# Cross attention with eight-slot batches: residual rows in four buffers loaded one per slot, and all query-weight sums on GpSimd

## The chip, the cores and the metric

The kernel runs on one core of one Trainium2 chip. The metric is device time in microseconds (us), the median of several executions. The core has five instruction queues that run beside each other and wait for one another by semaphores: TensorE (PE, matrix products into PSUM), VectorE (DVE), ScalarE (ACT), GpSimd (POOL) and SyncE (SP). In this kernel almost every DMA is issued by SP. Each queue is worked off in its order.

## The reference

All is float32: x is 8 x 256 x 1024, the context is 8 x 256 x 1024, there are 32 heads of width 32.

```python
residual = x
h = (x - mean(x)) * rsqrt(var(x) + 1e-5) * ln_gamma + ln_beta
Q = split_heads(h @ Wq.T)                       # 32 heads of 32
K = V = split_heads(ctx)
scores = where(mask, einsum(Q, K) / sqrt(32), -inf)
attn = einsum(softmax(scores), V)
out = residual + merge_heads(attn) @ Wout.T
```

## The kernel before

**Slots.** The work is cut into 64 slots, n = 0 to 63: eight per batch (NQ = 8), each with four heads. The main loop (line 828) writes the instructions of each slot in a fixed order; nothing reorders them afterwards. In slot n TensorE does the scores of slot n + 1 (`scores`, L469), the product of probabilities and values of slot n - 2 (`values`, L599), a part of the query projection of a later batch (L330 and, from batch 3 on, L430), and a part of the output projection of the batch before (L661). The softmax of slot n + 1 runs beside it: VectorE adds the mask bias and takes the minimum (L503), ScalarE takes the exponential (L507), VectorE the reciprocal of the sum (L514), GpSimd multiplies (`normalize`, L516, 8 instructions a slot), VectorE transposes by blocks (`blocks`, L522), ScalarE copies a part (L528), and SP moves blocks between partitions (L579, L583). I write b for the batch whose output is projected and i for the place in its eight slots: n = 8(b + 1) + i.

**Output projection with seven products.** The output of a batch is made by a Strassen-like scheme of seven products (`PRODUCTS`, L624) instead of eight, 28 matmuls in all, spread over the slots by `STEPS` (L631; the last such batch by `ENDS`). All go to one PSUM bank, since `ps_o` has one buffer. The first product, A11 with B11, is copied aside (`keep_p1`, L669). After A12 with B21 has been added, the bank is added to the residual rows (0,0) and stored: `store`, L682 on VectorE and L683 on SP, in slot i = 2. Only then may the next product that begins the bank, S2 with T2, start on TensorE. In the same way `store(1, 0)` in slot 6 comes before the product S1 with T1. `take` (L678) adds the bank to other residual rows in slots 3 and 4, and GpSimd adds the first product to three of the four residual tiles (`add_p1`, L673, in slots 2 to 4). In the batch that `ENDS` governs (slots 56 to 63) the additions to the residual stand ahead of the slot's softmax; otherwise they are hooks within the softmax, after its eight L503 (hook 0) or a little later (hook 1).

**Residual rows.** A residual tile is 128 rows by 512 columns of x, 256 KB, read from DRAM by `load_res` (L148) into the pool `rp`, which has three buffers. The four tiles of a batch are called (s, h). The loads are put into the list `between`, which SP issues within the slot's tail between the two pairs of probability moves. With three buffers a load waits until the tile three places before has been stored:

```python
for s, h in {1: ((0, 0), (0, 1)), 2: ((1, 1),), 3: ((1, 0),)}.get(i, ()):
    between.append(partial(load_res, b, s, h))
```

**Query weights.** From batch 3 (`SPLIT`) the query projection also uses seven products. Its combined weights T1 to T4 are made once, in slots 9 to 21, from the blocks of Wq by 16 additions of 128 x 512 (`sum_wq`, L381), eight on GpSimd and eight on VectorE. T1 goes into the tile `ring`; T3, T2 and T4 replace blocks of `wq` that are used up. B11, T1 and T3 are written to DRAM (`keep_wq`, L387 and L390) and loaded into `ring` in every later batch (`load_ring`, L397). The same kind of sums for the output weights, `sum_wo` (L183), is on GpSimd.

**The rest.** `load_mask` (L189) and `mask_bias` (L459) prepare one batch's mask, each with two buffers. `sum_at` (L651) and `sum_x` (L420) are the GpSimd sums on the data side of the seven products.

Of the kernel before, what the change touches and what calls it, by code (L numbers as in the profile page):

```python
# [46 lines left out]
F32 = mybir.dt.float32  # L47
U8 = mybir.dt.uint8
# [3 lines left out]
P = 128  # L52
# [7 lines left out]
def xattn_kernel(  # L60
# [11 lines left out]
    nc = tc.nc  # L72
    B, S, D = x.shape
    T = mask.shape[2]
    HD = D // HEADS
    NC = D // P
    NQ = NC
# [10 lines left out]

    const = ctx.enter_context(tc.tile_pool(name="const", bufs=1))
    xp = ctx.enter_context(tc.tile_pool(name="xp", bufs=2))  # L90
    rp = ctx.enter_context(tc.tile_pool(name="rp", bufs=3))
    lnp = ctx.enter_context(tc.tile_pool(name="lnp", bufs=2))
    kp = ctx.enter_context(tc.tile_pool(name="kp", bufs=2))
    vp = ctx.enter_context(tc.tile_pool(name="vp", bufs=2))
# [5 lines left out]
    sm = ctx.enter_context(tc.tile_pool(name="sm", bufs=8))  # L100
# [4 lines left out]
    ps_q = ctx.enter_context(tc.tile_pool(name="ps_q", bufs=1, space=PS))  # L105
    ps_o = ctx.enter_context(tc.tile_pool(name="ps_o", bufs=1, space=PS))

    ident = const.tile([P, P], F32, tag="ident", name="ident")
    make_identity(nc, ident)
    mhalf = const.tile([P, NS], F32, tag="mhalf", name="mhalf")  # L110
    nc.gpsimd.memset(mhalf, -0.5)
# [34 lines left out]
    def load_res(b, s, h):  # L146
# [5 lines left out]
    gs = const.tile([P, NC], F32, tag="gs", name="gs")  # L152
    qa = const.tile([P, NQ, S + 1], F32, tag="qa", name="qa")
    wq = const.tile([P, NC, NC, P], F32, tag="wq", name="wq")
    NK = NC // 2
    ring = const.tile([P, NK, NK, P], F32, tag="ring", name="ring")
    sums_x = const.tile([P, 2, NK, NA, K], F32, tag="sx", name="sx")
    kept = {
        name: dram.tile([P, NK, NK * P], F32, tag=name, name=f"kept_{name}")
        for name in ("T1", "B11", "T3")  # L160
    }
    wo = const.tile([P, 7, NK, 512], F32, tag="wo", name="wo")
    B11, B21, B22, T1, T2, T3, T4 = range(7)
# [5 lines left out]
    def load_wo(which, pair):  # L169

        k, h = {B11: (0, 0), B21: (1, 0), B12: (0, 1), B22: (1, 1)}[which]
        rows = woT[ds((NK * k + 2 * pair) * P, 2 * P), ts(h, 512)]
        nc.sync.dma_start(
# [11 lines left out]
    mks = {}  # L185

    def load_mask(b):
        mks[b] = sm.tile([P, T], U8, tag="mk", name=f"mk_{b}", bufs=2)
        nc.sync.dma_start(mks[b], mask[:, b].to_broadcast([P, T]))  # L189

    nc.scalar.dma_start(gam, gamma)
# [4 lines left out]
    load_wq(0)  # L196
    load_k(0)
    load_mask(0)
    load_x(1, 0)
    load_wq(1)  # L200
# [162 lines left out]
    SPLIT = 3  # L363
    SOON, LATE = 0, NK
    W_AT = {"B12": (SOON, 0), "B22": (SOON, NK), "B11": (LATE, 0), "B21": (LATE, NK),
            "T2": (SOON, 0), "T3": (SOON, 0), "T4": (LATE, 0)}

    def weights(name, o):

        if name == "ring":  # L370
            return ring[:, o]
        first, k = W_AT[name]
        return wq[:, first + o, ds(k, NK)]

    def sum_wq(to, o, engine):

        to, a, b, op = {
            "T1": ("ring", "B12", "B11", ALU.subtract), "T3": ("T3", "B22", "B12", ALU.subtract),
            "T2": ("T2", "T3", "B11", ALU.add), "T4": ("T4", "B21", "T2", ALU.subtract),
        }[to]  # L380
        engine.tensor_tensor(weights(to, o), weights(a, o), weights(b, o), op)  # L381

    def keep_wq(name, half):

# [69 lines left out]
    mbs, scs, pTs, pvs, ats, pos = {}, {}, {}, {}, {}, {}  # L454

    def mask_bias(b):

        mbs[b] = sm.tile([P, T], F32, tag="mb", name=f"mb_{b}", bufs=2)
        nc.vector.tensor_scalar(mbs[b], mks.pop(b), 1.0, -MASKED, ALU.subtract, ALU.mult)  # L459

    def scores(n, part=range(NS)):
# [182 lines left out]
    def sum_at(b, name):  # L644
        if name == "S2":
            s2s[b] = up.tile([P, NK, P], F32, tag="s2", name=f"s2_{b}")
        one, two, op = {
            "S3": ("A11", "A21", ALU.subtract), "S2": ("A22", "S3", ALU.subtract),
            "S1": ("S2", "A11", ALU.add), "S4": ("A12", "S2", ALU.subtract),
        }[name]  # L650
        nc.gpsimd.tensor_tensor(operand(b, name), operand(b, one), operand(b, two), op)  # L651
# [54 lines left out]
    for n in range(N):  # L706
# [8 lines left out]
    loads, stats, norms, trans, moves, biases, masks = (  # L715
        {n: [] for n in range(N)} for _ in range(7)
    )
    for b in range(1, B):
        first = NQ * (b - 1) + 2
        if b == 1:  # L720
            when = dict(moves=())
        elif b == 2:
            when = dict(
                loads=(0, 1), stats=(2, 3), norms=(3, 3), trans=(4, 4),
                moves=tuple(4 + i // 4 for i in range(16)),
            )
        else:
            when = dict(
                loads=(first - 12, first - 11), stats=(first - 10, first - 9),
                norms=(first - 8, first - 7), trans=(first - 7, first - 6),  # L730
                moves=tuple(first - 5 + i // 6 for i in range(16)),
            )
        for table, key in (
            (loads, "loads"), (stats, "stats"), (norms, "norms"), (trans, "trans"),
        ):
            for i, n in enumerate(when.get(key, ())):
                assert n < first
                table[n].append((b, i))
        for n in range(N):
            part = [i for i, slot in enumerate(when["moves"]) if slot == n]  # L740
            if part:
                assert n < first - 1
                moves[n].append((b, part))
        biases[NQ * b - 3].append(b)
        masks[NQ * b - 5].append(b)


    sums = {n: [] for n in range(N)}
    for n, which, *chunks in (
        (3, T3, 0), (4, T3, 1), (5, T2, 0), (6, T2, 1), (7, T3, 2), (8, T3, 3), (8, T2, 2),  # L750
        (9, T2, 3), (11, T4, 0, 1), (12, T4, 2, 3), (12, T1, 0), (13, T1, 1, 2), (14, T1, 3),
    ):
        sums[n] += [partial(sum_wo, which, c) for c in chunks]
    for n, which, o, engine in (
        (9, "T1", 0, nc.gpsimd), (12, "T1", 1, nc.vector), (13, "T1", 2, nc.vector),
        (14, "T1", 3, nc.gpsimd), (14, "T3", 0, nc.gpsimd), (14, "T3", 1, nc.vector),
        (15, "T3", 2, nc.gpsimd), (15, "T3", 3, nc.vector), (16, "T2", 0, nc.gpsimd),
        (17, "T2", 1, nc.vector), (19, "T2", 2, nc.gpsimd), (19, "T2", 3, nc.vector),
        (20, "T4", 0, nc.gpsimd), (20, "T4", 1, nc.vector), (21, "T4", 2, nc.gpsimd),
        (21, "T4", 3, nc.vector),  # L760
    ):
        sums[n].append(partial(sum_wq, which, o, engine))


    away, rings = {n: [] for n in range(N)}, {n: [] for n in range(N)}
    for n, name, half in (
        (9, "B11", 0), (10, "B11", 1), (13, "T1", 0), (15, "T1", 1), (15, "T3", 0), (16, "T3", 1),
    ):
        away[n].append(partial(keep_wq, name, half))
    for n, b in firsts.items():  # L770
# [14 lines left out]
    ln_norm(0, 1, nc.vector)  # L785
    first_q(0, early + late)
    mask_bias(0)
    transpose_x0(1)
    scores(0, (0,))
# [19 lines left out]
    for b in range(B - 1):  # L809
        done, ends = 0, b == B - 2  # L810
        for i, counts in enumerate(ENDS if ends else STEPS):
            n = NQ * (b + 1) + i
# [15 lines left out]
    for n in range(N):  # L828
        b, i = divmod(n - NQ, NQ)
        new_q = new_qs[n]  # L830
        between = []
# [3 lines left out]
            between.append(partial(load_k, n + 4))  # L835
        between += rings[n]
        if b >= 0:
            for s, h in {1: ((0, 0), (0, 1)), 2: ((1, 1),), 3: ((1, 0),)}.get(i, ()):
                between.append(partial(load_res, b, s, h))
        between += [partial(load_x, *args) for args in loads[n]]  # L840
        between += [partial(load_mask, one) for one in masks[n]]
        if n < NQ:
            which, pair = (
                (B12, 0), (B22, 0), (B11, 0), (B12, 1), (B22, 1), (B11, 1), (B21, 0), (B21, 1)
            )[n]
# [54 lines left out]
        for one in biases[n]:  # L900
            mask_bias(one)
        project_steps(n, 2)
        if b >= 0:
            for name in {0: ("S3",), 2: ("S4",), 4: ("S1",)}.get(i, ()):
                sum_at(b, name)
        for slot, name in ((n + 2, "S1"), (n + 1, "S2"), (n + 1, "S4"), (n - 1, "S3")):
            if slot in firsts:
# [12 lines left out]
        if not new_qs[n] and n - 2 > N - NQ:  # L920

            chunks = [c for c in range(NQ) if N - NQ + c <= n - 3]
# [65 lines left out]
```

## Time and profile before

| | |
|---|---|
| median of 3 runs | 637.47 us (635.39 to 637.86) |
| the profiled execution, its time | 635.33 us |
| its span in the trace | 633.5 us |
| mean granted TensorE clock in it | 0.967 |
| busy: PE | 587.1 us (93%) |
| busy: DVE | 468.1 us (74%) |
| busy: ACT | 411.6 us (65%) |
| busy: POOL | 381.6 us (60%) |
| residual loads, issue to landing, median | 4.7 us by the list of issues |

Busy time of an engine is the time in which it worked on an instruction; a wait is idle time just before an instruction, and the profile names what released it. All durations come from the one profiled execution, whose time is 1.8 us above its span and 2.1 us below the median. The clock row of the profile gives the share of full TensorE speed that was granted in each fortieth of the span (15.8 us each).

### The profile page before, as it was taken

To read this page: it belongs to the slowest core of one execution; us is meant where nothing else is said; L and a number is where in the kernel's file an instruction comes from. 1 tells how busy PE (TensorE), PEld (TensorE's weight loads), DVE (VectorE), ACT (ScalarE), POOL (GpSimd) and SP (SyncE) were. 2 spreads that over 40 slices of the span, in tenths; PEclk is the share of its full clock that TensorE was granted. 3 is DMA by queue.
4 is the path that set the end of the run, shared out by engine and by line. 5 is a ranking of instruction groups with operands and counts; after the bars stand their busy time and mean duration, and the time that the engine had idled before them with its cause. 6 is when DMAs were issued, how large, how long until landed. Compare 5 with 4: busy or idle time off the path is not lost.

```text
span 633.5 us, 19986 instructions
## 1 busy us (share of the span) xinstructions
PE 587.1 (93%) x7160; PEld 399.5 (63%) x7160; DVE 468.1 (74%) x1698; ACT 411.6 (65%) x1420; POOL 381.6 (60%) x651
## 2 busy tenths in 40 slices
PE   8999999798999999799997999799997999958897
PEld 7787685465666766477665777457764676624343
DVE  6878777789868887688786888668765677748801
ACT  4778875775667676687747866677655766636710
POOL 1667976797587945765467734776446554546500
PEclk9999799999999999899998999989998999969899
DMA  8566786655876668576766678755766664446441
GB/s 317 184 200 187 189 250 173 213 165 155 227 246 187 190 189 241 174 220 196 207 205 178 188 215 234 216 159 155 192 178 211 205 166 127 142 134 184 114 139 66
DMA packets 48483, 119.02 MB, mean 188 GB/s; under 512 B 10240, under 2 KB 10240, under 8 KB 48384
## 3 DMA queue, kind: packets, MB, share of 16 engines
q1 hardware_dynamic: 48096, 117.74, 62.7%
q8 instruction: 57, 0.93, 0.7%
q14 instruction: 42, 0.34, 0.2%
q10 hardware_dynamic: 288, 0.01, 0.0%
HBM read 66.33 MB, written 11.53 MB: 123 GB/s over the span
## 4 chain that ended last, share of the span: by engine, by line
PE 54%; POOL 14%; DMA 10%; DVE 9%; issue 6%; ACT 4%; SPq 3%; DVEq 0%; POOLq 0%; ACTq 0%
PE po_S L661 14%; PE pq_A L430 13%; POOL e L516 10%; PE sc L469 7%; PE pv L599 6%; PE po_A L661 4%; DVE e L503 4%; DMA r<-in_x_dram 4%; PE po L690 3%; PE pq L330 3%; PE pq_S L430 3%; DMA pT<-pc 2%; ACT e L507 2%; DVE pT L522 2%; SPq L579 2%
## 5 line engine op out<-in xcount | busy, mean ns | idle before, releaser
L516 POOL TENSOR_SCALAR e<-e,rden 128x256 f32<-128x256 f32 x512 | 236.1, 478 | 174.2 <-DVE rden L514 171.8
L507 ACT ACTIVATE e<-e,mn 128x256 f32<-128x256 f32 x512 | 254.0, 501 | 60.0 <-DVE mn L503 57.9
L522 DVE STREAM_TRANSPOSE pT<-e 128x512 f32<-128x512 f32 x256 | 180.8, 707 | 44.6 <-POOL e L516 33.9
L503 DVE CUSTOM_DVE_ANT_0 e<-sc,mb 128x256 f32<-128x256 f32 x512 | 185.1, 416 | 37.5 <-PE sc L469 37.5
L528 ACT COPY pc<-pT 128x512 f32<-128x512 f32 x128 | 79.1, 618 | 94.8 <-DVE pT L522 52.3
L507 ACT ACTIVATION_READ_ACCUMULATOR e<-e,mn 128x1 f32 x512 | 98.1, 192 | 0.0
L661 PE MATMUL po_S<-wo,s 128*128 128x512 f32 x112 | 64.5, 708 | 34.3 <-DVE rden L514 24.2
L330 PE MATMUL pq<-xnT,wq 128*128 128x256 f32 (+1 forms) x368 | 86.2, 389 | 1.2 <-ACT qa L337 1.2
L661 PE MATMUL po_S<-wo,at 128*128 128x512 f32 x168 | 81.7, 606 | 1.8 <-DVE r L678 1.8
L330 PEld LDWEIGHTS pq<-xnT,wq 128*128 128x128 f32 x368 | 70.2, 194 | 16.4 <-issue 3.9
L599 PE MATMUL pv<-pT,v 64*32 64x128 f32 x4096 | 75.7, 276 | 2.6 <-ACT qa L339 1.4
L469 PE MATMUL sc<-k,qa 32*128 32x256 f32 x1024 | 77.3, 412 | 0.1
L469 PEld LDWEIGHTS sc<-k,qa 32*128 32x128 f32 x1024 | 48.1, 190 | 46.2 <-issue 27.1
L599 PEld LDWEIGHTS pv<-pT,v 64*32 64x32 f32 x4096 | 58.1, 106 | 28.7 <-issue 15.9
L661 PEld LDWEIGHTS po_S<-wo,s 128*128 128x128 f32 x112 | 22.4, 220 | 57.5 <-issue 51.1
L661 PE MATMUL po_A<-wo,at 128*128 128x512 f32 x112 | 53.2, 609 | 0.2 <-ACT qa L339 0.2
L514 DVE RECIPROCAL rden<-den 128x2 f32<-128x2 f32 x256 | 38.2, 149 | 20.1 <-ACT e L507 18.4
L661 PEld LDWEIGHTS po_S<-wo,at 128*128 128x128 f32 x168 | 28.6, 190 | 25.0 <-issue 22.0
L503 DVE DVE_READ_ACCUMULATOR2_ANT mn<- 128x1 f32 x512 | 42.1, 82 | 0.0
L430 PEld LDWEIGHTS pq_A<-xnT,wq 128*128 128x128 f32 x320 | 37.3, 192 | 4.8 <-issue 4.8
L430 PE MATMUL pq_A<-xnT,wq 128*128 128x128 f32 x320 | 37.3, 275 | 0.0
L661 PEld LDWEIGHTS po_A<-wo,at 128*128 128x128 f32 x112 | 19.7, 189 | 22.0 <-issue 19.9
(77 smaller groups left out, 588.9 us busy)
## 6 DMA issues: line engine op xcount, KB each, us to landing
v<-in_kv_dram SPq DMA_DIRECT2D x32, 512.0 KB, 4.1
pT<-pT SPq DMA_DIRECT2D x128, 128.0 KB, 2.4
pT<-pc SPq DMA_DIRECT2D x128, 128.0 KB, 4.5
ring<-kept_T SPq DMA_DIRECT2D x18, 512.0 KB, 6.0
k<-in_kv_dram SPq DMA_DIRECT2D x32, 256.0 KB, 3.3
x<-in_x_dram SPq DMA_DIRECT2D x14, 512.0 KB, 6.0
r<-in_x_dram SPq DMA_DIRECT2D x28, 256.0 KB, 4.7
out_dram<-r SPq DMA_DIRECT2D x28, 256.0 KB, 3.3
```

The costliest lines, as they stand in the source:

```text
L330: nc.tensor.matmul(pqs[n], wq[:, o, c, :], xnTs[b](c), start=(c == 0), stop=(c == NC - 1),)
L430: nc.tensor.matmul(pqs[b][:, o, :], w[:, c], x_[:, c], start=begins and o + c == 0, stop=c == NK - 1, skip_group_check=True,)
L469: nc.tensor.matmul(scs[n][j][:, s, :], qa[r, n % NQ, ts(s, P)], ks[n - n % 2][r, n % 2, :], start=True, stop=True,)
L503: nc.vector.tensor_tensor_reduce(out=e[:, s, :], in0=pss[j][:, s, :], in1=mbs[n // NQ], scale=1.0, scalar=NO_SCORE, op0=ALU.add, op1=ALU.m ...
L507: nc.scalar.activation(e[:, s, :], e[:, s, :], AF.Exp, bias=mn[:, s : s + 1], scale=-1.0, accum_out=den[:, s : s + 1],)
L514: nc.vector.reciprocal(rden, dens[j])
L516: nc.gpsimd.tensor_scalar(es[j][:, s, :], es[j][:, s, :], rden[:, s : s + 1], 1.0, ALU.mult, ALU.mult,)
L522: nc.vector.transpose(pT[:, :, :, j, :, :].rearrange("p a i s k -> p (a i) s k"), es[j].rearrange("p s (b t) -> p b s t", t=K),)
L528: nc.scalar.copy(pc[:, :, ts(j, 2)], pT[:, 1, :, ts(j, 2)])
L599: nc.tensor.matmul(pvs[n][r][j * HD : (j + 1) * HD], vs[n - n % 2][ts(r, 2 * K), i, ds(n % 2 * P + j * HD, HD)], pT[ts(r, 2 * K), :, i, j, ...
L661: nc.tensor.matmul(pos[b], operand(b, name)[:, c], wo[:, which, c], start=begins and c == 0, stop=c == NK - 1, skip_group_check=not begins,)
L690: nc.tensor.matmul(po, ats[b, k][:, i, s].rearrange("p a k -> p (a k)"), w[:, i], start=(c == 0), stop=(c == NC - 1),)
```

## The change

1. The pool of residual tiles gets a fourth buffer, and each of the slots i = 0 to 3 of a batch issues one load: (0,0), (0,1), (1,1), (1,0). The tile (0,0) is so loaded one slot earlier; the others stay in their slots. With four buffers a load waits for the store of the same tile of the batch before.
2. To make room in SBUF the mask and the mask bias have one buffer each, and the identity matrix lies in the first 128 columns of `ring`, which is free until slot 9. The mask is loaded two slots earlier (slot 8b - 7) and its bias made one slot later (8b - 2).
3. All 16 sums of query weights are on GpSimd, most of them later: three of them in each of the slots 15 and 20, two in 14, 21 and 22. Two of the output-weight sums (T4) move one slot ahead. The writes of T1 and of T3 to DRAM follow their sums.
4. The sum S1 for the output (`sum_at`) moves from slot i = 4 to i = 5, but for the last batch that uses it.

```diff
-    rp = ctx.enter_context(tc.tile_pool(name="rp", bufs=3))
+    rp = ctx.enter_context(tc.tile_pool(name="rp", bufs=4))
...
-    ident = const.tile([P, P], F32, tag="ident", name="ident")
+    NK = D // P // 2
+    ring = const.tile([P, NK, NK, P], F32, tag="ring", name="ring")
+    ident = ring[:, 0, 0, :]
...
-        mks[b] = sm.tile([P, T], U8, tag="mk", name=f"mk_{b}", bufs=2)
+        mks[b] = sm.tile([P, T], U8, tag="mk", name=f"mk_{b}", bufs=1)
...
-        engine.tensor_tensor(weights(to, o), weights(a, o), weights(b, o), op)
+        nc.gpsimd.tensor_tensor(weights(to, o), weights(a, o), weights(b, o), op)
...
-        mbs[b] = sm.tile([P, T], F32, tag="mb", name=f"mb_{b}", bufs=2)
+        mbs[b] = sm.tile([P, T], F32, tag="mb", name=f"mb_{b}", bufs=1)
...
-        biases[NQ * b - 3].append(b)
-        masks[NQ * b - 5].append(b)
+        biases[NQ * b - 2].append(b)
+        masks[NQ * b - 7].append(b)
...
-        (9, T2, 3), (11, T4, 0, 1), (12, T4, 2, 3), (12, T1, 0), (13, T1, 1, 2), (14, T1, 3),
+        (9, T2, 3), (10, T4, 0), (11, T4, 1, 2), (12, T4, 3), (12, T1, 0), (13, T1, 1, 2),
+        (14, T1, 3),
...
-        (9, "T1", 0, nc.gpsimd), (12, "T1", 1, nc.vector), (13, "T1", 2, nc.vector),
-        (14, "T1", 3, nc.gpsimd), (14, "T3", 0, nc.gpsimd), (14, "T3", 1, nc.vector),
-        (15, "T3", 2, nc.gpsimd), (15, "T3", 3, nc.vector), (16, "T2", 0, nc.gpsimd),
-        (17, "T2", 1, nc.vector), (19, "T2", 2, nc.gpsimd), (19, "T2", 3, nc.vector),
-        (20, "T4", 0, nc.gpsimd), (20, "T4", 1, nc.vector), (21, "T4", 2, nc.gpsimd),
-        (21, "T4", 3, nc.vector),
...
+        (9, "T1", 0), (14, "T1", 1, 2), (15, "T1", 3), (15, "T3", 0, 1), (16, "T3", 2),
+        (18, "T3", 3), (19, "T2", 0), (20, "T2", 1, 2, 3), (21, "T4", 0, 1), (22, "T4", 2, 3),
...
-        (9, "B11", 0), (10, "B11", 1), (13, "T1", 0), (15, "T1", 1), (15, "T3", 0), (16, "T3", 1),
+        (9, "B11", 0), (10, "B11", 1), (15, "T1", 0), (16, "T1", 1), (16, "T3", 0), (19, "T3", 1),
...
-            for s, h in {1: ((0, 0), (0, 1)), 2: ((1, 1),), 3: ((1, 0),)}.get(i, ()):
-                between.append(partial(load_res, b, s, h))
+            if i < 4:
+                between.append(partial(load_res, b, *((0, 0), (0, 1), (1, 1), (1, 0))[i]))
...
-            for name in {0: ("S3",), 2: ("S4",), 4: ("S1",)}.get(i, ()):
+            for name in {0: ("S3",), 2: ("S4",), 4 if b == B - 2 else 5: ("S1",)}.get(i, ()):
```

More of the change, by code (lines that the diff above doesn't have):

```diff
@@ L154, in xattn_kernel @@
     wq = const.tile([P, NC, NC, P], F32, tag="wq", name="wq")
-    NK = NC // 2
-    ring = const.tile([P, NK, NK, P], F32, tag="ring", name="ring")
     sums_x = const.tile([P, 2, NK, NA, K], F32, tag="sx", name="sx")
@@ L373, in weights, with sum_wq @@
         return wq[:, first + o, ds(k, NK)]
-    def sum_wq(to, o, engine):
+    def sum_wq(to, o):
         to, a, b, op = {
@@ L750, in xattn_kernel @@
         (3, T3, 0), (4, T3, 1), (5, T2, 0), (6, T2, 1), (7, T3, 2), (8, T3, 3), (8, T2, 2),
-        (9, T2, 3), (11, T4, 0, 1), (12, T4, 2, 3), (12, T1, 0), (13, T1, 1, 2), (14, T1, 3),
+        (9, T2, 3), (10, T4, 0), (11, T4, 1, 2), (12, T4, 3), (12, T1, 0), (13, T1, 1, 2),
+        (14, T1, 3),
     ):
         sums[n] += [partial(sum_wo, which, c) for c in chunks]
-    for n, which, o, engine in (
-        (9, "T1", 0, nc.gpsimd), (12, "T1", 1, nc.vector), (13, "T1", 2, nc.vector),
-        (14, "T1", 3, nc.gpsimd), (14, "T3", 0, nc.gpsimd), (14, "T3", 1, nc.vector),
-        (15, "T3", 2, nc.gpsimd), (15, "T3", 3, nc.vector), (16, "T2", 0, nc.gpsimd),
-        (17, "T2", 1, nc.vector), (19, "T2", 2, nc.gpsimd), (19, "T2", 3, nc.vector),
-        (20, "T4", 0, nc.gpsimd), (20, "T4", 1, nc.vector), (21, "T4", 2, nc.gpsimd),
-        (21, "T4", 3, nc.vector),
+    for n, which, *chunks in (
+        (9, "T1", 0), (14, "T1", 1, 2), (15, "T1", 3), (15, "T3", 0, 1), (16, "T3", 2),
+        (18, "T3", 3), (19, "T2", 0), (20, "T2", 1, 2, 3), (21, "T4", 0, 1), (22, "T4", 2, 3),
     ):
-        sums[n].append(partial(sum_wq, which, o, engine))
+        sums[n] += [partial(sum_wq, which, o) for o in chunks]
     away, rings = {n: [] for n in range(N)}, {n: [] for n in range(N)}
     for n, name, half in (
-        (9, "B11", 0), (10, "B11", 1), (13, "T1", 0), (15, "T1", 1), (15, "T3", 0), (16, "T3", 1),
+        (9, "B11", 0), (10, "B11", 1), (15, "T1", 0), (16, "T1", 1), (16, "T3", 0), (19, "T3", 1),
     ):
```

## The prediction

> **What bounds the kernel now.** The page comes first: TensorE is busy for 93% of the span, in most slices for 90% and more, and the chain that ended last is mostly TensorE's. So a gain must come out of TensorE's idle time or its clock. The rows by slice show where both are low together.
>
> ```profile
> PE 587.1 (93%) x7160; PEld 399.5 (63%) x7160; DVE 468.1 (74%) x1698; ACT 411.6 (65%) x1420; POOL 381.6 (60%) x651
> ...
> PE   8999999798999999799997999799997999958897
> ...
> PEclk9999799999999999899998999989998999969899
> ```
>
> The idle time is 633.5 - 587.1 = 46.4 us. The list of waits, TensorE's rows and then VectorE's, says who ended it.
>
> ```profile
> PE po_S L661 <- DVE rden L514: 24.2, 8, 4.2
> PE po_S L661 <- DVE r L682: 10.1, 2, 7.6
> ...
> DVE r L682 <- DMA r<-in_x_dram: 13.0, 4, 6.8
> ...
> DVE r L682 <- issue: 9.6, 3, 4.7
> ```
>
> The columns are the total, the number of waits and the longest. Nearly all is the start of a new product in the one PSUM bank (po_S). The reciprocal that is named is only the last event of VectorE before it; what TensorE needs is L682, which empties the bank. L682 itself waited seven times, 13.0 + 9.6 = 22.6 us, and L682 on po_A is exactly the seven `store(0, 0)` of slots 10, 18, ... 58. The timeline of slot 26, by engine (start, duration, instruction, in brackets the idle time before it), shows the order.
>
> ```profile
> 256.82 3.73 PE L430 MATMUL pq_S<-sx,ring 128*128 128x128 f32 x32
> 264.32 3.58 PE L661 MATMUL po_S<-wo,s 128*128 128x512 f32 x4 [3.77 <-DVE rden L514]
> 267.84 1.15 PE L469 MATMUL sc<-k,qa 32*128 32x256 f32 x16
> ...
> 260.74 0.42 DVE L503 CUSTOM_DVE_ANT_0 e<-sc,mb 128x256 f32<-128x256 f32 x1
> 263.49 0.69 DVE L682 TENSOR_TENSOR r<-po_A,r 128x512 f32<-128x512 f32 x1 [2.32 <-DMA r<-in_x_dram]
> ...
> 259.25 0.92 SPq L148 DMA_DIRECT2D r<-in_x_dram  x2
> ```
>
> SP issued the row load at 259.25 and L682 began at 263.49, 4.2 us later; VectorE stood still for 2.32 us with the rest of the softmax behind it, and TensorE for 3.77. In slots 34, 42 and 50, where the trace names no releaser ("issue"), the loads went out at 333.00, 406.63 and 482.81 and L682 began at 337.15, 411.27 and 487.04, again 4.2 to 4.6 us later. So these are the same wait.
>
> **Change 1, rows (0,0) a slot earlier.** A slot is 8.5 to 9.5 us, and of L682's wait at most 6.76 us lies behind the load. Issued a slot earlier it has landed; I take the waits to be gone. Without them L682 starts when VectorE is free, and TensorE 0.83 us after that (264.32 - 263.49). TensorE gains the smaller of VectorE's wait and its own idle time:
>
> slot 10: wait 2.27, idle 3.83, gain 2.27. Slot 18: 1.66, 1.64, 1.64. Slot 26: 2.32, 3.77, 2.32. Slot 34: 2.23, 3.68, 2.23. Slot 42: 2.72, 4.17, 2.72. Slot 50: 4.66, 4.20, 4.20. Slot 58: 6.76, 7.60, 6.76. Sum **22.1 us**.
>
> What is late next in slots 26, 34 and 42 is L682 behind its eight L503, which began only after the layer norm's L223: 1.45 us of TensorE's idle time stay in each.
>
> The clock comes on top. After the stops of slots 26 to 50 TensorE ran slow: po_S x4 took 3.58, 2.47, 3.75 and 3.75 us instead of 1.96 (slot 18), and the scores behind it up to 2.09 instead of 1.15. The granted clock in these stretches was 0.74 (265 to 270), 0.76 (338 to 345), 0.68 (412 to 421) and 0.69 (488 to 496). The losses by slot are 1.6, 1.6, 2.8 and 2.4, in sum 8.4 us, all ahead of work in which TensorE is never idle, and VectorE then waited 1.0 to 2.3 us for the scores. After an idle time of 1.64 us (slot 18) the clock was 1.00. The Trainium skill, page "TensorE: Matmul & The Clock Gate", section "What's actually happening", has half speed after an idle window of about 3.4 us and full speed after a busy one; by this rule each dip would cost half of one window, 1.7 us, in sum 6.8. The window runs freely, which fits slot 10: idle for 3.83 us and 1.00 after it. I take the rows, **8.4 us**; the page agrees that a remainder of 1.45 us costs no clock. In slot 58 I count nothing for the clock: there GpSimd's L673, not TensorE, sets the next step.
>
> SP's queue: in slot i = 0 the load now stands behind k (256 KB), for b >= 3 two ring loads of 512 KB, and ahead of the second pair of probability moves (L583). It costs these one issue of 0.44 us. Their cover: the probabilities moved at 198.8 in slot 18 are read by L599 at 220.6 in slot 21, some 15 us after landing. If that cover were gone, each batch would pay 0.44. The row load there has until slot i = 2. Its own buffer wait is for a store one batch old. Tile (0,1), still loaded in slot 1, now waits for the store of slot 0 for which (0,0) waited before; it is needed in slot 2's L673. Tile (1,0) no longer waits for the store of slot 2. Tile (1,1) stays behind the ring loads of slot 2, and L673's wait of 1.71 us for it in slot 19 stays.
>
> **Change 2, mask and identity.** Eight mask loads (0.43 us of SP each) and eight biases (0.27 to 0.72 us of VectorE) move and none is added. The single buffers cost no wait: the bias is made on VectorE behind the last reader of the old one on the same queue, and the mask load of slot 8b - 7 waits for a bias made three slots before. Nothing is read from `ring` as a weight before slot 9. I cost this at nothing; what covers SP is its waiting for ScalarE's copies in every slot. If it is not covered, it is 0.43 us a batch.
>
> **Changes 3 and 4, sums to GpSimd.** VectorE loses eight sums, 6 x 0.91 + 2 x 1.49 = 8.4 us, and GpSimd gains eight of 1.27 us, 10.2 us. Here a rule speaks against the change: the Trainium skill, page "GPSIMD Engine Reference", section "4.1 Engine selection", wants elementwise sums on VectorE, GpSimd being about half as fast with two inputs. The trace agrees with the ratio for an undisturbed sum: 1.27 on GpSimd, 0.65 on VectorE. But side by side they spoil one another:
>
> ```profile
> 213.99 1.73 POOL L381 TENSOR_TENSOR wq<-wq 128x512 f32<-128x512 f32 x1
> 216.83 3.78 POOL L516 TENSOR_SCALAR e<-e,rden 128x256 f32<-128x256 f32 x8 [1.11 <-DVE rden L514]
> ...
> 213.36 1.23 DVE L381 TENSOR_TENSOR wq<-wq 128x512 f32<-128x512 f32 x1
> ```
>
> By the rule the change would cost 10.2 - 8.4 = 1.8 us, and up to 10.2 if GpSimd were the bound; by the rows each sum moved takes VectorE's off a chain and goes into GpSimd's wait for the next reciprocal, like the 1.11 above. I compare slot by slot what is added with the idle time of GpSimd before the next L516. Slot 15: two sums, 2.54, in 2.79. Slot 18: 1.27 in 1.18. Slot 20: two more, but S1 gone and the 0.46 of contention gone, 0.8 in 1.11. Slot 21: one and S1, 2.54 in 2.99. Slot 22: 2.54 in 3.52. Slot 13: S1, 1.27 in 2.79. Slot 10: 1.27 in 1.17. So nearly all fits. Two things follow for TensorE:
>
> A gain: in slot 14 the product S1 waited 2.31 us (152.10) for L682, and 0.62 us in slot 22 (226.17). Ahead of slot 14's L682 VectorE did the sums of 1.23 (137.0) and 1.75 (146.8), the bias of 0.72, and a wait of 1.51 for GpSimd behind three output-weight sums, of which one and S1 leave slot 12. That is more than 2.31; in slot 22 the bias of 0.52 and a sum of 0.68 leave. **2.9 us**.
>
> A loss: in slot 21 TensorE began the product with T2 at 214.16, its four weight blocks 0.93 us apart. GpSimd now makes three of these at the end of slot 20: from L673's end at 212.8 (S1 gone) they would be ready at 214.1, 215.4 and 216.7, needed at 215.1, 216.0 and 216.9. That has no slack once TensorE gains on GpSimd; between 0 and three sums (3.8) I take **1.5**, one sum and some contention, since TensorE and GpSimd both start from the same earlier L682. T4 (slot 22, read in slot 23) has over 1 us.
>
> The sum against the profiled execution: 635.33 - 22.1 - 8.4 - 2.9 + 1.5 = 603.4. It stands 2.1 us below the median of the runs, so **605.5 us** for the median.
>
> **The rivals.** *The waits go, the clock stays low.* If the remaining 1.45 us and TensorE's small gaps still drop the clock, the 8.4 is not had: 635.3 - 22.1 - 2.9 + 1.5 + 2.1 = 614. For it: four of seven stops dropped it. Against it: 1.64 and 2.31 us did not.
>
> *GpSimd becomes the bound in slots 14 to 22.* If the sums do not fit, since normalize is late and with it VectorE's transposes, up to the whole 10.2 comes back and the 2.9 is not had: 605.5 + 13.1 - 1.5 = 617. For it: the chain already runs through GpSimd between 135 and 186. Against it: the idle times listed.
>
> *Slower: L682 does not wait for the rows.* In three of seven stops the trace names no releaser, and TensorE is put down to the reciprocal. If L682 waited for something else of its slot, the earlier load brings nothing, and the moved sums cost: GpSimd's 10.2 less at most the 2.9, 637.5 + 7.3 = 645. It decides where L682 starts after the change: if it still starts over 2 us after its last L503 with the rows long landed, this is it. Against it: the 4.2 to 4.6 us from issue to start in all of them, the same as the landing time.
>
> *Nothing changes*, the load being issued earlier but landing as late because of the ring loads ahead of it: slots 10 and 18 have none ahead of them (b < 3), and 1.25 MB at the 200 GB/s of these slices takes 6 us, with a slot and a half at hand.
>
> **How the numbers follow.** Forecast 0.72, the clock rival 0.13, GpSimd 0.08, slower 0.04, nothing 0.03. The likeliest gives 605.5. The unknowns in it (0 to 3.8 for T2, 6.8 to 8.4 for the clock, VectorE limiting by a microsecond or two, the 2.1 between profile and median) make 601 to 611. For 8 in 10 the range goes to the clock rival and most of the GpSimd case above, and a little below the forecast for idle time that vanishes wholly: 598 to 617. A measurement of this kernel can tell about 0.5%, 3.2 us, from no change. Faster 0.93, same 0.03, slower 0.04.
>
> **What would show it.** Right: L682 on po_A without a wait for the rows; TensorE's po_S waits about 12 us in place of 36; granted clock near 1.00 behind slots 26 to 50; no L381 on VectorE and its L381 on GpSimd all near 1.27; VectorE busy some 8 us less, GpSimd some 10 more. Wrong: L430 waiting for GpSimd in slot 21 by more than 2 us, L522 waiting for GpSimd more in 150 to 230, or a new wait for L583's moves.

## The result, and the profile after

The changed kernel takes 599.64 us (median of 4 runs, 598.71 to 602.04); the kernel before, run beside it, takes 637.26 us. The ratio is 0.942, with a 95% interval of 0.9384 to 0.9456. That is 37.6 us less, and 5.9 us below the forecast of 605.5. Its profiled execution took 602.04 us, the slowest of the four, with a span of 600.3 us and a mean granted clock of 0.989 (0.967 before).

The page of the changed kernel, the same rows as were shown of before:

```profile
PE 577.5 (96%) x7160; PEld 396.5 (66%) x7160; DVE 460.1 (77%) x1690; ACT 410.8 (68%) x1420; POOL 391.2 (65%) x659
...
PE   9998999999999999999998999999999999978997
...
PEclk9998999999999999999999999999999999989899
```

TensorE's idle time is 600.3 - 577.5 = 22.8 us, where it was 46.4. Its busy time fell by 9.6 us although it issues the same 7160 matmuls: that goes with the clock, whose seven near the start and four eights in the middle of the span are gone. VectorE is busy 8.0 us less and GpSimd 9.6 us more, as the moved sums should give.

The list of waits of the changed kernel (total, times, longest). The rows of GpSimd and VectorE come ahead of TensorE's here:

```profile
POOL r L673 <- DMA r<-in_x_dram: 16.1, 8, 5.2
...
PE po_S L661 <- DVE rden L514: 4.6, 4, 1.5
...
PE po_S L661 <- DVE r L682: 3.6, 2, 2.9
...
PE po_S L661 <- DVE r L678: 3.3, 1, 3.3
...
PE pq_S L430 <- DMA ring<-kept_T: 1.4, 2, 1.3
```

The waits of TensorE for the PSUM bank behind VectorE's reciprocal and L682 fell from 24.2 + 10.1 to 4.6 + 3.6 us. L678's 3.3 is one single stop, the longest left. The three rows make 11.5 us, where about 12 was forecast. Two rows are ones to remember: GpSimd's L673 now waits 16.1 us for residual rows (5.7 before), and there is a new wait of TensorE for `ring`. Among VectorE's groups of the changed kernel (busy time, mean ns of one, idle time just before it) L682 on po_A has no idle time at all; it had 22.6 us:

```profile
L682 DVE TENSOR_TENSOR r<-po_A,r 128x512 f32<-128x512 f32 x7 | 4.8, 681 | 0.0
```

Slot 26 of the changed kernel, by engine:

```profile
247.52 3.73 PE L430 MATMUL pq_S<-sx,ring 128*128 128x128 f32 x32
252.64 1.96 PE L661 MATMUL po_S<-wo,s 128*128 128x512 f32 x4 [1.38 <-DVE rden L514]
254.52 1.15 PE L469 MATMUL sc<-k,qa 32*128 32x256 f32 x16
...
251.46 0.42 DVE L503 CUSTOM_DVE_ANT_0 e<-sc,mb 128x256 f32<-128x256 f32 x1
...
251.81 0.69 DVE L682 TENSOR_TENSOR r<-po_A,r 128x512 f32<-128x512 f32 x1
```

L682 starts as soon as the last L503 is done, and TensorE 0.83 us after L682's start (252.64 - 251.81). What is left is 1.38 us, 1.45 having been foreseen. The four matmuls take 1.96 instead of 3.58 us.

### The profile page after: what moved, and what is told of

It reads as the page before. It is cut to its first block, busy times and chain, and to the rows that moved or that the text cites. A ratio compares the mean times of both kernels' runs of the same rounds, so it can differ in the third digit from the quotient of the medians.

```text
span 600.3 us, 19985 instructions
## 1 busy us (share of the span) xinstructions
PE 577.5 (96%) x7160; PEld 396.5 (66%) x7160; DVE 460.1 (77%) x1690; ACT 410.8 (68%) x1420; POOL 391.2 (65%) x659
## 4 chain that ended last, share of the span: by engine, by line
PE 67%; POOL 11%; DMA 7%; DVE 7%; ACT 3%; issue 2%; SPq 2%; POOLq 0%; DVEq 0%; ACTq 0%
PE po_S L661 17%; PE pq_A L430 13%; PE pq L330 9%; PE sc L469 8%; POOL e L516 8%; PE pv L599 7%; PE po_A L661 4%; PE po L690 3%; DVE e L503 3%; PE pq_S L430 3%; DMA r<-in_x_dram 2%; ACT e L507 2%; DMA pT<-pc 1%; DMA ring<-kept_T 1%; DVE st L223 1%
## 5 line engine op out<-in xcount | busy, mean ns | idle before, releaser
L516 POOL TENSOR_SCALAR e<-e,rden 128x256 f32<-128x256 f32 x512 | 237.4, 482 | 117.7 <-DVE rden L514 114.9
L522 DVE STREAM_TRANSPOSE pT<-e 128x512 f32<-128x512 f32 x256 | 181.2, 708 | 48.1 <-POOL e L516 44.1
L503 DVE CUSTOM_DVE_ANT_0 e<-sc,mb 128x256 f32<-128x256 f32 x512 | 185.0, 416 | 24.7 <-PE sc L469 24.5
L661 PE MATMUL po_S<-wo,at 128*128 128x512 f32 x168 | 83.4, 617 | 3.3 <-DVE r L678 3.3
L330 PEld LDWEIGHTS pq<-xnT,wq 128*128 128x128 f32 x368 | 69.6, 192 | 16.1 <-issue 4.6
L469 PEld LDWEIGHTS sc<-k,qa 32*128 32x128 f32 x1024 | 46.1, 184 | 42.4 <-issue 16.2
L469 PE MATMUL sc<-k,qa 32*128 32x256 f32 x1024 | 73.6, 400 | 0.1
L661 PE MATMUL po_S<-wo,s 128*128 128x512 f32 x112 | 57.1, 637 | 8.1 <-DVE rden L514 4.6
L503 DVE DVE_READ_ACCUMULATOR2_ANT mn<- 128x1 f32 x512 | 42.6, 83 | 0.0
L661 PEld LDWEIGHTS po_S<-wo,s 128*128 128x128 f32 x112 | 20.3, 199 | 28.0 <-issue 17.9
L673 POOL TENSOR_TENSOR r<-r,p 128x512 f32<-128x512 f32 x21 | 26.9, 1280 | 16.2 <-DMA r<-in_x_dram 16.1
```

Source lines behind the costliest of these rows:

```text
L330: nc.tensor.matmul(pqs[n], wq[:, o, c, :], xnTs[b](c), start=(c == 0), stop=(c == NC - 1),)
L469: nc.tensor.matmul(scs[n][j][:, s, :], qa[r, n % NQ, ts(s, P)], ks[n - n % 2][r, n % 2, :], start=True, stop=True,)
L503: nc.vector.tensor_tensor_reduce(out=e[:, s, :], in0=pss[j][:, s, :], in1=mbs[n // NQ], scale=1.0, scalar=NO_SCORE, op0=ALU.add, op1=ALU.m ...
L516: nc.gpsimd.tensor_scalar(es[j][:, s, :], es[j][:, s, :], rden[:, s : s + 1], 1.0, ALU.mult, ALU.mult,)
L522: nc.vector.transpose(pT[:, :, :, j, :, :].rearrange("p a i s k -> p (a i) s k"), es[j].rearrange("p s (b t) -> p b s t", t=K),)
L661: nc.tensor.matmul(pos[b], operand(b, name)[:, c], wo[:, which, c], start=begins and c == 0, stop=c == NK - 1, skip_group_check=not begins,)
```

## The experiments

The theory is that of the prediction: a late row load stops VectorE, VectorE keeps the bank from TensorE, and a stop of TensorE costs clock on top; the moved sums are worth a few us. Against it stand three rivals: that the room in SBUF and the moved masks carry part of the gain; that the low clock belongs to these places of the program and not to the stops; and that the fourth buffer, not the earlier issue, is what counts. The later runs ask what the waits that are left are worth. Where an expectation speaks of theories A and B, they are those of that run. The kernel before was timed beside each of the three groups of runs (medians 637.75, 635.99 and 636.18 us); gains are against the one beside it.

**The loads alone** (changes 1 and 2; sums, their writes and S1 as before). The edit against the kernel before, without the lines of change 2:

```diff
-    rp = ctx.enter_context(tc.tile_pool(name="rp", bufs=3))
+    rp = ctx.enter_context(tc.tile_pool(name="rp", bufs=4))
...
-            for s, h in {1: ((0, 0), (0, 1)), 2: ((1, 1),), 3: ((1, 0),)}.get(i, ()):
-                between.append(partial(load_res, b, s, h))
+            if i < 4:
+                between.append(partial(load_res, b, *((0, 0), (0, 1), (1, 1), (1, 0))[i]))
```

> The loads in four slots with the fourth buffer, and the room made for it (changes 1 and 2); the 16 sums of query weights and the sum S1 stay where they were before. My theory: nearly all of the gain is the seven waits of store(0,0) for its rows and the clock behind them, 22.1 + 8.4 us, so some 605 to 609 us, and TensorE's waits of 2.3 us in slot 14 and 0.6 us in slot 22 are still there. Rival (the moved sums carry a large part, since VectorE is late in slots 12 to 22): 615 us or more. No L682 on po_A waits for rows under either.

Measured: 606.46 us, ratio 0.9507 (0.947 to 0.9543), a gain of 31.3 us. The loads and the clock are most of the change, and L682 on po_A has no idle time before it. TensorE still stops in slot 14 (1.49 us), in slot 22 (1.13), and in slot 18 too (1.56), where the prediction had put the whole stop to the rows.

**The sums alone** (changes 2, 3 and 4, the old loads and three buffers). The edit against the changed kernel:

```diff
-    rp = ctx.enter_context(tc.tile_pool(name="rp", bufs=4))
+    rp = ctx.enter_context(tc.tile_pool(name="rp", bufs=3))
...
-            if i < 4:
-                between.append(partial(load_res, b, *((0, 0), (0, 1), (1, 1), (1, 0))[i]))
+            for s, h in {1: ((0, 0), (0, 1)), 2: ((1, 1),), 3: ((1, 0),)}.get(i, ()):
+                between.append(partial(load_res, b, s, h))
```

> The sums on GpSimd at their new places and the room (changes 2, 3 and 4), with three row buffers and the loads of before. My theory: the waits of L682 on po_A stay, only the waits in slots 14 and 22 go (2.9 us) and a little in slot 21 is lost: 633 to 636 us. Rival (GpSimd becomes the bound with 10.2 us more): 640 us or more, with L522 waiting for L516 in slots 14 to 22. Second rival (the sums carry a large part of the gain): 625 us or less.

Measured: 631.61 us, 0.9896 (0.9853 to 0.9939), a gain of 6.1 us, more than was expected; its one profile is shorter by 4.0 us (span 629.5). TensorE has no stop in slots 14 and 22 there, and in slot 18 one of 0.22 us instead of 1.64, though L682 still waits 2.17 us for its rows in that slot. The two gains, 31.3 + 6.1, make 37.4 of the whole 37.6: by the medians the parts hardly help or hinder one another. L682's waits for rows stay, as VectorE's group shows:

```profile
L682 DVE TENSOR_TENSOR r<-po_A,r 128x512 f32<-128x512 f32 x7 | 4.8, 691 | 23.4 <-DMA r<-in_x_dram 13.8 <-issue 9.5
```

**Three buffers** in the changed kernel:

```diff
-    rp = ctx.enter_context(tc.tile_pool(name="rp", bufs=4))
+    rp = ctx.enter_context(tc.tile_pool(name="rp", bufs=3))
```

> The changed kernel with three row buffers instead of four. The load of (0,0) in slot i = 0 then has to wait for the store of (0,1) of the batch before, which is made in the same slot, and SP with it. My theory: what counts is that the load is issued a slot earlier; SP waits some 2 to 4 us in slot 0, the moves behind it have some 15 us to spare, and the time is within 3 us of the changed kernel, 598 to 604 us. Rival (the fourth buffer is what brings it, since a blocked SP makes the probabilities late): 610 us or more, with L599 waiting for DMAs of pT.

Measured: 599.86 us, 0.9406 (0.937 to 0.9442). The fourth buffer brings nothing that can be told, and the third rival falls.

**A stop filled with work** (the kernel before, with the product ahead of the stop made a second time in slots 26, 34, 42 and 50, 128 matmuls more in all). This is the test of the clock by itself:

```diff
         if n in products:
             query_product(*products[n])
+            if n in (26, 34, 42, 50):
+                query_product(*products[n])
```

> The kernel before, but in slots 26, 34, 42 and 50 TensorE makes the query product S1 twice (32 more matmuls in each, 3.6 us, the same values), in the time in which it stood still for L682. If the slow clock after these stops comes from TensorE's standing still, as I hold, it stays at full speed: po_S x4 in some 1.96 us, and the kernel with more work is faster by 8.4 us, 627 to 632 us. Rival (the clock falls for another reason, or the added work comes after the stop): 637 us or more and po_S still at 2.5 to 3.7 us.

Measured: 628.68 us, 0.9868 (0.9819 to 0.9918): 9.1 us less, with more work. The timeline of TensorE in slot 26 of this kernel:

```profile
258.40 7.63 PE L430 MATMUL pq_S<-sx,ring 128*128 128x128 f32 x64
265.86 1.95 PE L661 MATMUL po_S<-wo,s 128*128 128x512 f32 x4
267.74 1.15 PE L469 MATMUL sc<-k,qa 32*128 32x256 f32 x16
```

The rows are as late as before, but TensorE works in the time of the stop, and what follows runs in 1.95 and 1.15 us instead of 3.58 and up to 2.09. The windows behind slot 42's stop, first in the kernel before and then in this one; the number after the five busy times is the granted clock:

```profile
412.00:421.00 9.00, 8.90 (x91) 4.44 (x92) 5.77 (x24) 6.00 (x18) 6.15 (x11) 0.68 0.38 112
```

```profile
404.00:420.00 16.00, 15.49 (x173) 12.39 (x172) 11.71 (x50) 11.72 (x42) 11.54 (x19) 1.00 0.59 175
```

So the low clock came from the idle time ahead of it, and not from this place in the program; the second rival falls. Its slots 26 to 50 give 8.5 us by the traces, beside the 8.4 of the prediction.

**The room alone** (the kernel before with `ident` in `ring`, one buffer each for mask and bias, and their loads and biases in the new slots):

```diff
-        mks[b] = sm.tile([P, T], U8, tag="mk", name=f"mk_{b}", bufs=2)
+        mks[b] = sm.tile([P, T], U8, tag="mk", name=f"mk_{b}", bufs=1)
...
-        mbs[b] = sm.tile([P, T], F32, tag="mb", name=f"mb_{b}", bufs=2)
+        mbs[b] = sm.tile([P, T], F32, tag="mb", name=f"mb_{b}", bufs=1)
...
-        biases[NQ * b - 3].append(b)
-        masks[NQ * b - 5].append(b)
+        biases[NQ * b - 2].append(b)
+        masks[NQ * b - 7].append(b)
```

> Change 2 alone: identity in ring, one mask, one mask bias, the mask loaded two slots earlier and its bias made one slot later; sums, loads and three row buffers as before. Theory A (it is not neutral: every trace that holds it gains 5.9 us in slot 6 and loses 2.0 to 3.7 us in slot 4, some 2 us in all): 634 to 636 us. Theory B (it costs and brings nothing; what the traces show there is where the windows of TensorE's clock happen to fall): 637 us, and the one profile says no more than any other.

Measured: 637.79 us over 12 runs, 1.0025 (0.9991 to 1.0059). No effect that can be told: the room earns nothing by itself, and the first rival falls.

**The line of the loads alone** (the kernel before, three buffers, nothing else changed):

```diff
-            for s, h in {1: ((0, 0), (0, 1)), 2: ((1, 1),), 3: ((1, 0),)}.get(i, ()):
-                between.append(partial(load_res, b, s, h))
+            if i < 4:
+                between.append(partial(load_res, b, *((0, 0), (0, 1), (1, 1), (1, 0))[i]))
```

> The kernel before with one edit: one residual load in each of the slots 0 to 3, so (0,0) a slot earlier. Three buffers, two masks, sums on both engines, as before. Theory (the issue slot of this one load is the cause of the waits and, through them, of the slow clock): as the kernel with changes 1 and 2, 604 to 609 us. Rival (the fourth buffer or the mask's move is needed for it): 612 us or more.

Measured: 605.29 us, 0.9499 (0.945 to 0.9547), a gain of 30.9 us, that of change 1 with all its room. One load in each batch, issued one slot earlier, is about five sixths of the change. Its trace keeps a dip of the clock in slot 42 (another stands at the end, in slot 59):

```profile
397.45 3.46 PE L661 MATMUL po_S<-wo,s 128*128 128x512 f32 x4 [2.15 <-DVE rden L514]
```

**Odd sums on VectorE** (the changed kernel's times and places, only the engine of every second sum changed):

```diff
     def sum_wq(to, o):
 
+        engine = nc.vector if o % 2 else nc.gpsimd
...
-        nc.gpsimd.tensor_tensor(weights(to, o), weights(a, o), weights(b, o), op)
+        engine.tensor_tensor(weights(to, o), weights(a, o), weights(b, o), op)
```

> The changed kernel with the sums of query weights at their new places, but those of odd index (8 of 16) on VectorE. It tells the engine from the place. My theory: the two engines' sums lengthen each other again (1.2 to 1.7 us instead of 0.65 and 1.27) and VectorE's come ahead of its softmax: slower than the changed kernel by 1 to 3 us, 600.5 to 603 us. Rival (GpSimd was too full, the places matter and not the engine): 597 to 599 us.

Measured: 601.29 us, 0.9462 (0.9413 to 0.9511). It lies 1.6 us above the changed kernel's median, but the intervals overlap: the times do not settle whether the engine or the new places of the sums earn their 6.1 us. Its trace says more. The sums lengthen one another again (1349 ns on GpSimd and 924 on VectorE in the mean for those into `wq`), and yet TensorE has no stop in slots 14 and 18, and one of 0.69 us in slot 22, where the loads alone left 1.49, 1.56 and 1.13. So in this one trace the new places, S1's among them, account for most of those stops, and the engine for at most the 0.69.

**L682 ahead of the slot's L503** in all batches, to take the remaining waits of about 1.4 us:

```diff
-            elif one == B - 2:
+            elif one == B - 2 or (what is store and i == 2):
```

> The changed kernel with L682 of store(0,0) ahead of the slot's eight L503 in all batches (before only in the last). Theory: the remaining 1.4 us of TensorE's idle time in slots 10, 26, 34 and 42 (4.6 us in the trace after the change) are L682's place behind the L503; they go, and nothing else changes: 595 to 597 us. Rival (TensorE meets the later softmax a slot on, since VectorE is then 0.65 us behind, or L682 waits for the product and holds the softmax): 599 us or more.

Measured: 599.64 us, 0.9447 (0.9394 to 0.95), beside 599.64 and 599.69 for the changed kernel in two other groups: no gain. TensorE gains 1.6 to 1.9 us at the start of slots 10, 26 and 34 and gives 0.8 to 1.6 back within two slots, where the trace now has it wait for L678. In slot 42 it gains 0.65 and gives back 2.2. L682, which now comes earlier, waits for its rows again in slots 26 to 50, 3.7 us in all. In slot 27:

```profile
258.10 1.98 PE L661 MATMUL po_S<-wo,at 128*128 128x512 f32 x4 [0.56 <-DVE r L678]
```

**More loads earlier** (the edit above, T1 of `ring` one slot earlier, and in the last batch the rows earlier and L673 ahead of L651):

```diff
-        for slot, name in ((n - 2, "T1"), (n, "B11"), (n + 2, "T3")):
+        for slot, name in ((n - 3, "T1"), (n, "B11"), (n + 2, "T3")):
...
-            if i < 4:
-                between.append(partial(load_res, b, *((0, 0), (0, 1), (1, 1), (1, 0))[i]))
+            late = ((0, 0), (0, 1), (1, 1), (1, 0))
+            for s, h in (late[:1], late[1:3], late[3:])[i] if b == B - 2 and i < 3 else () if b == B - 2 else late[i : i + 1]:
+                between.append(partial(load_res, b, s, h))
...
+        if b == B - 2 and i in (2, 3, 4):
+            add_p1(b, *{2: (0, 1), 3: (1, 1), 4: (1, 0)}[i])
...
-        if b >= 0 and i in (2, 3, 4):
+        if 0 <= b < B - 2 and i in (2, 3, 4):
```

> The changed kernel with four more edits: L682 of store(0,0) ahead of the L503; ring's T1 loaded one slot earlier (TensorE waited 1.25 us for it in slot 34); rows (1,1) and (1,0) of the last such batch one slot earlier (GpSimd waited 0.69 us); and in that batch the L673 ahead of the sums L651. Theory: besides the 4.6 us of the former kernel, 1.2 us in slot 34, and in the slots 59 to 62 TensorE's waits of 3.3 and 2.9 us shrink by 1.2 to 1.7 each: 590 to 594 us. Rival (the last batch is bound by its chain of softmax steps whatever GpSimd does first): 595 us or more.

Measured: 606.04 us, 0.9531 (0.9479 to 0.9583), 6 us slower than without these edits: a miss. The timeline around slot 34, SP, GpSimd and TensorE:

```profile
307.19 0.92 SPq L397 DMA_DIRECT2D ring<-kept_T  x2
...
310.71 2.54 SPq L317 DMA_DIRECT2D xnT<-xe  x4
...
318.50 1.26 POOL L420 TENSOR_TENSOR sx<-xnT 128x512 f32<-128x512 f32 x1 [5.05 <-DMA xnT<-xe]
...
326.50 3.63 PE L661 MATMUL po_S<-wo,s 128*128 128x512 f32 x4 [2.52 <-POOL rstd L229]
```

The 1 MB of T1 is issued ahead of the moves of xnT (L317). GpSimd's sum of the new batch's data, L420, then waits 5.05 us for these moves (1.60 in the changed kernel), with the slot's normalize behind it. VectorE's transpose, which needs the normalized tile, waits 4.25 us; L682 is late again, and the clock falls (3.63 us for four matmuls). TensorE's waits in this kernel's profile are put to `POOL rstd L229` for 5.9 us, a row that the changed kernel does not have. Beside the changed kernel's profile, TensorE loses 2.0 to 2.5 us in each of the slots 26, 34 and 42 with the slots just behind them, and the edits of the last batch win 4.6 us back at the end. So the edit that was meant to take away a wait of 1.25 us in slot 34 made longer ones. That the early T1 is the part that costs follows from the other parts, which cost nothing by themselves in the runs above and below; it was not run alone.

**The last batch alone** (the edit above without its first two lines and without the L682 edit):

> The changed kernel with two edits in its last eight-slot batch alone: rows (1,1) and (1,0) one slot earlier, and L673 ahead of the sums L651. Theory: TensorE's stops in slots 59 and 61 (3.3 and 2.9 us) shrink by 1.2 each, and the slow clock behind one of them may go: 596 to 598.5 us. Rival (nothing is won there, since L651 is then late for the product): 599 us or more.

Measured: 597.58 us, 0.9391 (0.936 to 0.9423), beside 599.69 us for the changed kernel. TensorE in slots 59 to 61 of this kernel:

```profile
534.52 3.70 PE L661 MATMUL po_S<-wo,at 128*128 128x512 f32 x8 [2.21 <-DVE r L678]
...
542.51 3.70 PE L661 MATMUL po_S<-wo,at 128*128 128x512 f32 x8 [1.27 <-DVE r L678]
...
551.00 3.70 PE L661 MATMUL po_S<-wo,s 128*128 128x512 f32 x8 [1.77 <-POOL s L651]
```

All three run at full speed; the changed kernel's first and third take 5.40 and 6.71 us in its first profile, 5.12 and 3.70 in the second. It is the fastest version found, but 2.1 us is at the edge of what the intervals separate.

**The changed kernel again**, unedited, as the mate of the last two:

> The changed kernel itself, beside the other two on the same chip: 598 to 601 us by both theories. In its profile I look at where the time differs from its first profile, which was the slowest of its four runs: if the difference lies in the slots 58 to 63 and 4 to 7, where TensorE stops and its clock falls by chance of the window, no other part of the account needs a change.

Measured: 599.69 us, 0.9426 (0.94 to 0.9453). Its profile (600.08 us) agrees with the first one (602.04 us) within 0.5 us everywhere up to slot 61, where its eight matmuls take 3.70 instead of 6.71 us; its span is 2.0 us shorter.

## Why the prediction was right, and where its sizes were off

The mechanism stood. L682's wait for the rows was the bound of these slots, the clock came back, and GpSimd took the sums. The measured 599.64 us lies within the wide range, 598 to 617, but below the narrow one, 601 to 611. The rival in which L682 does not wait for the rows fell with L682's group row above (0.0) and with the single line's 30.9 us; the rival of a clock that stays low fell with the granted 1.00 behind slots 26 to 50 (252.6 to 258, 323 to 330, 393 to 402 and 461.5 to 470 us); that the load lands as late as before fell with the same 0.0. The GpSimd rival fell too: GpSimd still waits 114.9 us for the reciprocal, and TensorE has no stop over 0.15 us between those of slots 10 and 26. One of the signs named for it did show: L522's wait for GpSimd rose from 33.9 to 44.1 us over the span, and in the slots of the sums from 7.1 to 10.3 (7.4 in the second profile). It did not reach TensorE.

How much earlier TensorE came in each place, worked out from the two profiled executions as the idle time and work lost in that slot before, less that after:

| place | predicted, us | measured, us |
|---|---|---|
| slot 10 | 2.27 | 2.34 |
| slots 14 and 22 (S1) | 2.9 | 2.55 + 0.86 |
| slot 18 | 1.64 | 1.87 |
| slot 21 (T2) | -1.5 | -0.25 |
| slot 26, wait and clock | 3.9 | 4.03 |
| slot 34 | 3.8 | 3.38 |
| slot 42 | 5.5 | 5.21 |
| slot 50 | 6.6 | 7.16 |
| slots 58 to 62 | 6.76 | 4.73 |
| sum | 31.9 | 31.9 |

That the sums are equal is luck; errors of both signs cancel. The clock's part in slots 26 to 50 came out at 8.5 us, where the prediction took the rows' 8.4 and not its estimate of 6.8 from the skill's page. Slot 18 agrees for another reason than the one given: the loads alone left 1.56 us of its stop (1.06 with the single line), the sums alone 0.22. With small gains elsewhere (the largest 2.2 us in slots 4 to 7) the two profiled times differ by 33.3 us.

*The largest miss is the correction of 2.1 us for the median.* The profile-based sum was 603.4, and the changed kernel's medians are 599.6 to 599.7. Of the 5.9 us, 2.1 is this correction: it assumed that the profile after stands below its median as the one before did, and this one stands 2.4 us above it. The other 3.8 us is that 2.4 and 1.4 us of terms. In the repeat the eight matmuls of slot 61 took 3.0 us less.

*The loss in slot 21 was mis-sized, 0.25 us for 1.5.* GpSimd's three sums and the product that reads them, in the changed kernel:

```profile
204.54 3.77 POOL L381 TENSOR_TENSOR wq<-wq 128x512 f32<-128x512 f32 x3
208.26 3.70 POOL L516 TENSOR_SCALAR e<-e,rden 128x256 f32<-128x256 f32 x8
...
205.55 3.98 PE L430 MATMUL pq_A<-sx,wq 128*128 128x128 f32 x32
```

The product started 1.0 us into the sums and took 3.98 us instead of 3.73: it ran just behind them. So the estimated times at which the blocks were ready and needed held nearly as they stood, and the allowance of 1.5 us on top was too much. GpSimd's L381 all came out near the 1.27 us of the prediction. The row is that of the twelve into `wq`; the four into `ring` took 1298 ns in the mean.

```profile
L381 POOL TENSOR_TENSOR wq<-wq 128x512 f32<-128x512 f32 x12 | 15.2, 1292 | 0.0
```

The rule weighed in the prediction, the Trainium skill, page "GPSIMD Engine Reference", section "4.1 Engine selection", holds for one undisturbed sum (0.65 us on VectorE, 1.27 on GpSimd), but did not decide here: the part of the change that moves all sums to GpSimd, and most of them to later slots, gained 6.1 us. It was predicted at 2.9 - 1.5 = 1.4 us, without slot 18; the runs of it spread over 627.92 to 633.68 us, and its profile gained 4.0, so the size is known to 2 or 3 us only.

*A wait in slot 34 was not foreseen.* TensorE with T1, and SP's issues ahead of it, in the changed kernel:

```profile
317.60 1.95 PE L430 MATMUL pq_S<-sx,ring 128*128 128x128 f32 x16
320.80 2.05 PE L430 MATMUL pq_S<-sx,ring 128*128 128x128 f32 x16 [1.25 <-DMA ring<-kept_T]
...
312.72 0.92 SPq L397 DMA_DIRECT2D ring<-kept_T  x2
```

The prediction asked whether the row load behind the ring loads would be in time, and it was; when T1 itself is needed was not asked. SP issued the ring loads only 4.9 us ahead of the product (7.8 us before), and the second half was 1.25 us late. This cost little: the stop that follows for L682 is 0.37 us in place of the 1.45 foreseen, and in the second profile the two are 0.35 and 1.11 us. So of the 1.25 us only some 0.2 could be won.

*The end was over-estimated, 4.73 us for 6.76.* L682's own step came 6.84 us earlier, but the rest of the chain did not follow. Slots 58 and 61 before:

```profile
562.31 6.49 PE L661 MATMUL po_S<-wo,s 128*128 128x512 f32 x8 [7.60 <-DVE r L682]
...
588.64 5.29 PE L661 MATMUL po_S<-wo,s 128*128 128x512 f32 x8 [2.48 <-DVE r L682]
```

Slots 58, 59 and 61 of the changed kernel:

```profile
527.24 3.67 PE L661 MATMUL po_S<-wo,s 128*128 128x512 f32 x8 [0.73 <-DVE r L682]
...
536.36 5.40 PE L661 MATMUL po_S<-wo,at 128*128 128x512 f32 x8 [3.29 <-DVE r L678]
...
554.29 6.71 PE L661 MATMUL po_S<-wo,s 128*128 128x512 f32 x8 [2.86 <-DVE r L682]
```

With the first stop gone TensorE meets L678 in slot 59 sooner and waits 3.29 us for it (0.48 before), since L678 waits for GpSimd's L673, which stands behind the slot's normalize and L651. Over slots 58 to 61 the stops fell from 11.8 us (with 0.48 and 1.27 in slots 59 and 60) to 6.9, so by 4.9 and not by 6.8. The prediction counted nothing for the clock here. Against 3.70 us for eight matmuls it cost 2.8 and 1.6 us before and 1.7 and 3.0 after; that the two nearly cancel is chance, since the second profile of the changed kernel does not have the 3.0.

GpSimd's L673 in slot 61 waits 0.69 us for its rows and hands this on to L682. Of the other waits of L673 for rows, 15.4 us, none ends in a stop of TensorE, though VectorE's L678 waits 4.4 us behind them in slots 20, 28, 36 and 52.

## What to carry to other kernels

Where one PSUM bank is shared, ask which instruction empties it and what that instruction waits for: the trace named the reciprocal, and the cause was a 256 KB load issued 4.2 us ahead of its use. A short wait on VectorE can cost TensorE twice, once as a stop and once as clock, so the time to take away is found by adding both; filling the stop with useless work is a cheap test of the second half. And a load may be moved earlier only past things that can wait: one load of 256 KB in each batch, one slot earlier, was worth 31 us, while 1 MB ahead of SP's moves was part of an edit that cost 6.

## What was not expected of the hardware

- Whether a stop costs clock is not told by its length alone. In slot 10 a stop of 3.83 us cost nothing in the kernel before, while one of 3.93 us with the filled stops and one of 4.18 us with the sums alone made the four matmuls there take 3.75 us instead of 1.96. The stop of 2.15 us in slot 42 of the one-line kernel cost 1.5 us (3.46 for 1.96), with a granted clock of 0.72 over the 6 us behind it. In slot 61 of the changed kernel, stops of 2.86 and 2.41 us in two executions were followed by 6.71 and 3.70 us for the same eight matmuls; there a stop of 2.48 us was followed by 5.29 us in the kernel before and by 3.70 with odd sums on VectorE. The idle window of about 3.4 us in the rule weighed in the prediction (the Trainium skill, page "TensorE: Matmul & The Clock Gate", section "What's actually happening") does not foretell this: stops of 2.15 to 3.29 us cost clock here, while the remainders of up to 1.5 us cost none.
- Sums of two inputs on VectorE and GpSimd slow one another: GpSimd's took 1422 ns in the mean with VectorE's beside them, and 1292 ns without them; VectorE's own took 1062 ns, where an undisturbed one took 0.65 us. The rows are those of the loads alone:

```profile
L381 POOL TENSOR_TENSOR wq<-wq 128x512 f32<-128x512 f32 x6 | 8.5, 1422 | 1.3 <-DMA kept_T<-wq 1.3
...
L381 DVE TENSOR_TENSOR wq<-wq 128x512 f32<-128x512 f32 x6 | 6.4, 1062 | 0.0
```

- Slots 4 and 6 differ between the profiles. Near 52 to 55 us TensorE waits 2.4 to 3.3 us for a DMA in every kernel with change 2, and 0.7 to 0.9 in the three without it, a cost that the prediction put at nothing. From 66 to 78 us the kernel before was granted a clock of 0.72, every other kernel 1.00, with change 2 or without it. Change 2 by itself came out neutral in 12 runs.
- Still open: how much of the 6.1 us of the sums is the engine's; why one stop costs clock and another of the same length does not; and whether the last-batch version is truly faster than the changed kernel.
